# One more block of a GRU step by seven products instead of eight, in a four-layer graph network on one core

## The chip, the cores and the metric

The kernel runs on one core of a Trainium2 chip. A core has a matrix engine (PE, with its weight loads shown apart as PEld), a vector engine (DVE), an activation engine (ACT), a general engine (GpSimd, shown as POOL) and a queue from which transfers are issued (SP). Each engine works through its own queue in order; between engines semaphores hold an instruction until its inputs are there. The metric is device time in microseconds: 2803.21 us is the median of three runs of the kernel before (2800.3 to 2803.34).

## What is computed

128 graphs of 128 nodes with 256 features go through four layers, each followed by a layer normalisation of input plus output: an attention layer with four edge types, a mean-aggregation layer, three steps of a gated graph unit, and an attention layer. Cut to the third layer, which the change touches most:

```python
for i in range(3):
    m = h @ weight[i]
    aggr = A.T @ m                       # A = (adj != 0)
    gi = aggr @ w_ih.T + b_ih            # split in i_r, i_z, i_n
    gh = h @ w_hh.T + b_hh               # split in h_r, h_z, h_n
    r, z = sigmoid(i_r + h_r), sigmoid(i_z + h_z)
    n = tanh(i_n + r * h_n)              # the candidate; h_n is its state side
    h = (1 - z) * n + z * h
```

Everything is float32, with outputs of 128 x 128 x 256.

## The kernel before

Four graphs make a group (`G = 4`), 32 groups in all. Feature-major tiles hold 128 features on the partitions and the 512 nodes of a group in the columns (`T = 512`); 256 features are two such tiles (`KC = 2`). Per group the code records `loading`, `layer0`, `layer1`, `gru` with three calls of `step`, and `layer3`. The weights are prepared once in `weights`: `weight[i]` and `w_ih` are multiplied into `c_gi[i]`, so that a step needs only the aggregated state `agT` and the state `hT`.

**Order of the work.** Nothing is issued while it is recorded. Each operation becomes an `Op` with a cost, its predecessors and a nominal time (`paced`), and at the end of the file a planner issues them: at each turn it takes the engine that can start first, and on it, of the operations that are ready by its reckoning, the one with the earliest nominal time. `PERIOD` is the nominal distance of two groups; `EAGER` favours operations of the GRU on engines other than PE, `RUSH` the copies of `snapshot`; `HOP`, `PE_HOP` and `SLACK` are the margins that it adds between engines. Several groups are under way at once, so PE's queue mixes products of different groups and layers. All calls go to the engines through one helper, so every instruction of the trace carries line 232, and instructions are told apart by their tiles.

**A gate** (`gate`, line 701). A 256 x 256 weight block times the 256 x 512 state can be formed as 2 x 2 blocks. `direct` does this with products of 512 columns: two output banks, two products each. `gate` does it by Winograd's form of Strassen's scheme: seven products of 256 columns, with sums of weight blocks prepared in `w_s` and sums of state blocks formed by `sums` (on POOL for `hT`, tile `t_h`; on DVE for `agT`, tile `t_m`). Gates r and z add up state side and message side, so each of the seven is two products. The scheme accumulates products 1, 6, 7 and 4 in one PSUM bank, `shared`, and ACT copies it to SBUF after 1, 6 and 7 (`snapshot`, into quarters of `t_r` or `t_z`); products 5 and 3 go to a second bank, 2 to a third, and `plus` adds each to its quarter on DVE. A planner rule treats a PSUM bank as one thing: a product into a bank waits for whoever reads any part of it. There are eight banks, four under the tag `ps` and four under `gate`.

**The candidate.** Its state side is formed with `direct` into two banks of `ps`, and `hidden` moves them out with bias and factor 0.5 into tile `q`. Its message side is `direct` with `c_gi` and is added in `candidate`. `update` forms the new state, which `turned` and `back` turn into node-major form: DVE transposes 32 x 32 blocks into a tile `z_...`, SP stores it to DRAM and loads it back block-transposed. `turned_quick` does the same on PE and is used only in the first group and at the end.

**Normalising** (`normalise`, line 465). `statistics` gives mean and variance on DVE and the reciprocal root `rstd` on POOL. Graphs 0 and 2 of a group are then normalised on DVE and graphs 1 and 3 on ACT, in the tiles `xa`, `xb`, `xc` and `xd` of the four stages.

Of the kernel before, what the change touches and what calls it, by code (L numbers as in the profile page):

```python
# [18 lines left out]
def kernel(  # L19
# [219 lines left out]
    LANDING = 4.2  # L239
    HOP = 0.3  # L240
    PE_HOP = 1.0
    SLACK = 1.0

# [11 lines left out]
    def pool_cost(op, n, sums):  # L255
        return 1.56 if op in FAST else 0.55 if op == "memset" else 1.2 if n < 64 else 0.25 + n * 0.0023

# [7 lines left out]

    PERIOD = 92.637
    SPAN = 2.0
    EAGER, RUSH = 21.446, 39.26
    L0_START, L0_END, L1_START, L1_END, L3_START, L3_END = -2.0, -1.338, -0.867, -0.05, 0.05, 1.0
    H_END, M_START, M_END = 0.25, 0.12, 0.573  # L270

# [32 lines left out]

    w_s = tile_of("w_s", [P, NL + 1, 3, 2, P])

    def weights():
# [73 lines left out]
        for n in range(NL + 1):  # L381
            by = POOL if n > 1 else DVE
            w = [
                (w_hhT[:, k] if n == 0 else c_gi[:, n - 1, k])[:, : 4 * P].rearrange(
                    "p (g e x) -> p g e x", [P, 2, 2, P], g=2, e=2
                )
                for k in range(KC)
            ]
            a11, a12, a21, a22 = w[0][:, :, 0], w[1][:, :, 0], w[0][:, :, 1], w[1][:, :, 1]
            s2, s3, s4 = [w_s[:, n, j] for j in range(3)]  # L390
# [73 lines left out]

    def normalise(res, mv, rstd, tag):

        n = res.shape[1]
        nmr = tile_of(f"nmr_{tag}", [P, n], 2)
        DVE.scalar_tensor_tensor(nmr, mv[:, :, 0], -1.0, rstd, op0=OP.mult, op1=OP.mult)
        for b in range(0, n, 2):  # L470
            DVE.tensor_scalar(
                res[:, b, :], res[:, b, :], mv[:, b, 0:1], rstd[:, b : b + 1],
                op0=OP.subtract, op1=OP.mult,
            )
        for b in range(1, n, 2):
            ACT.activation(
                res[:, b, :], res[:, b, :], AF.Identity, bias=nmr[:, b : b + 1], scale=rstd[:, b : b + 1]
            )

    def softmax(alpha, tag, quick, tile=tile_of):  # L480

        n = alpha.shape[1]
        nmax = tile_of(f"nmax_{tag}", [P, n], 2)
        DVE.tensor_reduce(nmax, alpha, AX.X, OP.max, negate=True)
        p = tile(f"prob_{tag[0]}", [P, n, N])
        rs = tile_of(f"rsum_{tag}", [P, n], 2)
        for b in range(n):
            ACT.activation(
                p[:, b, :], alpha[:, b, :], AF.Exp, bias=nmax[:, b : b + 1], scale=1.0,
                accum_out=rs[:, b : b + 1],  # L490
            )
        rinv = tile_of(f"rinv_{tag}", [P, n], 2)
        DVE.reciprocal(rinv, rs)
        pT = tile(f"probT_{tag[0]}", [P, n, N])
        if quick:
            turned_quick(pT.rearrange(FLAT), [p[:, b, :] for b in range(n)])
        else:
            back(pT.rearrange(FLAT), turned(p, n, "p"))
        return pT, rinv
# [24 lines left out]
    def layer0(g, s):  # L524
# [39 lines left out]
        for h in range(G // 2):  # L564
# [5 lines left out]
            for j in range(2):  # L570
# [4 lines left out]
                )  # L575
        normalise(res, *statistics(res, "0"), "0")
        s.x1T = tile_of("x1T", [P, G, KC, N])
# [11 lines left out]
    def layer1(g, s):  # L589
# [17 lines left out]
        for b in range(G):  # L607
            ps = bank()
            PE.matmul(ps[:, : D + 1], a_f[:, b, :], hu[b][:, D:], start=True, stop=True)
            fac = tile_of("fac", [P, 1], 4)  # L610
            DVE.tensor_scalar_max(fac, ps[:, D : D + 1], 1.0)
            DVE.reciprocal(fac, fac)
            DVE.scalar_tensor_tensor(
                fac, ps[:, D : D + 1], 0.0, fac, op0=OP.is_gt, op1=OP.mult
            )
            DVE.scalar_tensor_tensor(
                res[:, b, :], ps[:, :D], fac, hu[b][:, :D], op0=OP.mult, op1=OP.add
            )
# [3 lines left out]
        normalise(res, *statistics(res, "1"), "1")  # L622

# [17 lines left out]
    def gru(g, s):  # L641
# [5 lines left out]
        def step(i, hT, parts):  # L647
# [30 lines left out]

            def sums(by, v, w, n, src, tag):

# [9 lines left out]
                def of(q):  # L690
                    block = lambda k, e: w[:, k, (q + e) * P : (q + e + 1) * P]
                    extra = lambda j: w_s[:, n, j, q // KC]
                    return {
# [6 lines left out]

            def gate(tag, q, sources):

                t = tile_of(tag, [P, 4, H])
                shared, other, last = bank("gate"), bank("gate"), bank("gate")

                def add(ps, p, first=False):
                    with PE:
                        for k, of in enumerate(sources):  # L710
                            PE.matmul(
                                ps[:, :H], *of(q)[p], start=(first and k == 0),
                                stop=(p in (2, 3, 4) and k == len(sources) - 1), skip_group_check=True,
                            )

                def snapshot(quarter):
                    ACT.copy(t[:, quarter], shared[:, :H])
                    ops[-1].rush = RUSH

                def plus(quarter, ps):  # L720
                    DVE.tensor_add(t[:, quarter], ps[:, :H], t[:, quarter])

                def tanh(out, in_, c):
                    ACT.activation(out, in_, AF.Tanh, bias=brz[:, q + c : q + c + 1], scale=0.5)

                add(shared, 1, True)
                snapshot(0)
                add(last, 2, True)
                plus(0, last)
                add(shared, 6)  # L730
                snapshot(1)
                add(other, 5, True)
                add(shared, 7)
                snapshot(3)
                plus(3, other)
                tanh(t[:, 3], t[:, 3], 1)
                add(shared, 4)
                tanh(t[:, 2], shared[:, :H], 1)
                add(other, 3)
                plus(1, other)  # L740
                halves = [t[:, 2 * c : 2 * c + 2].rearrange("p h n -> p (h n)") for c in range(KC)]
                tanh(halves[0], halves[0], 0)
                return halves[1], halves[0]

            def hidden(c, ps):
                t = tile_of("q", [P, T], 2)
                ACT.activation(t, ps, AF.Identity, bias=bhn[:, c : c + 1], scale=0.5)
                return t

# [34 lines left out]
            of_m = sums(DVE, agT, w_i, i + 1, agps, "t_m")  # L784
            t1, t0 = gate("t_r", R, (of_h, of_m))
            n1, d1 = candidate(1, direct(w_i, agT, C + 1), t1, q1)
            n0, d0 = candidate(0, direct(w_i, agT, C), t0, q0)
            z1, z0 = gate("t_z", Z, (of_h, of_m))
            update(1, z1, n1, d1)
# [11 lines left out]
        "rT": ("xs", 2), "xc": ("xa", 2), "wh": ("x_in", 1), "e": ("alpha0", 1), "alpha3": ("xT", 2),  # L801
        "prob_3": ("prob_0", 1), "probT_3": ("probT_0", 1), "xd": ("z_1", 1),
    }

    def layer3(g, s, first, last):
# [59 lines left out]
        pT, rinv = softmax(alpha, three, end, tile)  # L865
        normalise(x3, mv, rstd, two)

# [3 lines left out]
        for h in range(n // 2):  # L871
# [16 lines left out]
            )  # L888
        normalise(res, *statistics(res, three), three)
        SP.dma_start(out=out[g * G + first : g * G + last].rearrange("b n d -> n b d"), in_=res)  # L890
# [35 lines left out]
    def slot_at(buf, ahead=False):  # L926


        taken = slots.setdefault((buf.pool, buf.tag), [])
        done = sorted([b.free_at for b in taken if b.left == 0] + [0.0] * (buf.bufs - len(taken)))  # L930
        place = 0 if buf.pool is psum else buf.place.index(buf)
        return done[place] if place < (len(done) if ahead else min(1, len(done))) else None
# [96 lines left out]
```

## Time and profile before

| what | value |
|---|---|
| median of three runs | 2803.21 us |
| profiled execution, its own time | 2803.81 us |
| span of its profile (first to last instruction) | 2802.0 us |
| granted clock of PE, mean over the span | 0.990 |
| PE busy | 2741.4 us, 98% |
| DVE busy | 2351.3 us, 84% |
| ACT busy | 1552.1 us, 55% |
| POOL busy | 1349.1 us, 48% |
| traffic to and from HBM | 318.89 MB, 114 GB/s |

The page divides the span in 40 slices and gives, for each engine, tenths of busy time. The groups of instructions give a name as output tile, arrow, input tiles; for example `q<-ps,bhn` is the copy of the candidate's state side. The means that the page gives for matrix products overlap each other, because products are pipelined: the cost of a product is the distance between the starts of two that follow each other. Each product in float32 shows as two instructions.

The rows of the candidate's state side and of its copy out of PSUM are these, from the groups of instructions by form (busy us, mean ns of one, then idle time before):

| group | count | busy us | mean ns |
|---|---|---|---|
| PE `ps<-hT,w_hhT`, 512 columns | 512 | 242.3 | 601 |
| PE `ps<-h0T,w_hhT`, 512 columns | 256 | 115.9 | 593 |
| ACT `q<-ps,bhn`, 512 elements | 192 | 131.5 | 685 |
| DVE `xa<-xa,mv,rstd`, 256 elements | 64 | 50.1 | 791 |
| DVE `xb<-xb,mv,rstd`, 256 elements | 64 | 23.9 | 412 |

### The profile page before, as it was taken

The page shows a single profiled execution, that of the slowest core. Times are in us where ns is not written, and L with a number is a line of the kernel's source. Part 1 is how long each engine was busy: PE and PEld are TensorE (multiplying, and loading weights), DVE is VectorE, ACT ScalarE, POOL GpSimd, SP SyncE. Part 2 cuts the span into 40 slices and gives each one's busy share as a digit, 9 for nine tenths or more (in the row PEclk, how much of TensorE's full clock was granted, in tenths as well). Part 3 has the DMA queues.
Part 4 walks back from the last instruction along what each step waited for, and adds up shares of the span by engine and source line. Part 5 has one row for each costly group of instructions (what it writes and reads, how often), then busy time and mean ns, then how long its engine had stood idle before and what let it go on. Part 6 is the DMA issues. An engine that isn't in the chain of part 4 may idle for free.

```text
span 2802.0 us, 42709 instructions
## 1 busy us (share of the span) xinstructions
PE 2741.4 (98%) x13180; PEld 2030.5 (72%) x13180; DVE 2351.3 (84%) x5389; ACT 1552.1 (55%) x3512; POOL 1349.1 (48%) x1358
## 2 busy tenths in 40 slices
PE   8899999999999999999999999999999999999995
PEld 5677777777777777777777777777777777776663
DVE  5777889888888888889888888888888888888775
ACT  4454555555655555555555655555565555655554
POOL 4433545544455544555544455544555544454431
PEclk9999999999999999999999999999999999999996
DMA  5454556546555555555646555555555646555441
GB/s 118 107 105 98 118 125 129 113 99 132 121 125 126 115 107 125 121 125 124 120 100 131 118 126 127 115 109 124 117 126 126 119 101 131 108 116 117 95 87 48
DMA packets 1396626, 321.78 MB, mean 115 GB/s; under 512 B 1142064, under 2 KB 1387952, under 8 KB 1396400
## 3 DMA queue, kind: packets, MB, share of 16 engines
q1 hardware_dynamic: 1393952, 316.69, 54.0%
q10 hardware_dynamic: 2448, 2.36, 0.3%
q8 instruction: 107, 1.75, 0.3%
q14 instruction: 119, 0.97, 0.1%
HBM read 185.74 MB, written 133.15 MB: 114 GB/s over the span
## 4 chain that ended last, share of the span: by engine, by line
PE 95%; DVE 2%; ACT 1%; issue 1%; DMA 0%; POOL 0%; ACTq 0%; POOLq 0%; DVEq 0%
PE ps L232 54%; PE gate L232 41%; DVE t_r L232 0%; DVE rest L232 0%; DVE t_d L232 0%; ACT xs L232 0%; DMA acol<-in_L_gnn_a_dram 0%; DMA hn<-in_L_gnn_weight_dram 0%; ACT ps L232 0%; DVE xd L232 0%; POOL mk L232 0%; DVE hT L232 0%; DVE st L232 0%; DVE xb L232 0%; DVE t_z L232 0%
## 5 line engine op out<-in xcount | busy, mean ns | idle before, releaser
L232 PE MATMUL ps<-agT,c_gi 128*128 128x512 f32 x768 | 357.8, 592 | 0.0
L232 ACT COPY t_r<-gate 128x256 f32<-128x256 f32 x288 | 106.3, 369 | 348.4 <-PE gate L232 345.5
L232 POOL TENSOR_TENSOR rstd<-rstd,neg_half 128x4 f32<-128x4 f32 (+1 forms) x128 | 144.8, 1133 | 288.5 <-DVE rstd L232 281.0
L232 PEld LDWEIGHTS ps<-xs,xT 128*128 128x128 f32 x2048 | 247.8, 193 | 22.8 <-ACT agT L232 7.2
L232 PE MATMUL ps<-xs,xT 128*128 128x128 f32 x2048 | 253.3, 277 | 2.9 <-ACT xs L232 2.3
L232 PE MATMUL ps<-hT,w_hhT 128*128 128x512 f32 x512 | 242.3, 601 | 12.9 <-ACT wh L232 10.0
L232 POOL TENSOR_TENSOR t_d<-hT,t_n 128x512 f32<-128x512 f32 x128 | 173.1, 1353 | 164.3 <-ACT t_n L232 160.0
L232 PE MATMUL ps<-w_um,x1T 128*128 128x512 f32 x512 | 236.5, 594 | 2.2 <-ACT x1T L232 2.2
L232 PE MATMUL gate<-agT,c_gi 128*128 128x256 f32 x768 | 229.3, 380 | 1.4 <-ACT agT L232 1.4
L232 PE MATMUL gate<-t_h,w_hhT 128*128 128x256 f32 x768 | 229.0, 380 | 1.4 <-ACT t_z L232 1.4
L232 PE MATMUL gate<-t_m,c_gi 128*128 128x256 f32 x768 | 229.8, 381 | 0.0
L232 PE MATMUL gate<-t_h,w_s 128*128 128x256 f32 x768 | 228.5, 379 | 0.0
L232 PE MATMUL gate<-t_m,w_s 128*128 128x256 f32 x768 | 228.4, 379 | 0.0
L232 ACT ACTIVATE q<-ps,bhn 128x512 f32<-128x512 f32 x192 | 131.5, 685 | 171.5 <-PE ps L232 169.0
L232 PEld LDWEIGHTS ps<-agT,c_gi 128*128 128x128 f32 x768 | 145.8, 190 | 110.3 <-issue 101.2
L232 POOL TENSOR_TENSOR t_d<-h0T,t_n 128x512 f32<-128x512 f32 x64 | 86.0, 1344 | 281.0 <-ACT t_n L232 261.4
L232 ACT ACTIVATE xs<-xT,acol 128x512 f32<-128x512 f32 x256 | 173.9, 715 | 64.6 <-PE ps L232 58.3
L232 POOL TENSOR_SCALAR mk<-a_f 128x512 uint8<-128x512 f32 x128 | 193.5, 1519 | 15.3 <-DVE alpha L232 9.1
L232 DVE TENSOR_TENSOR t_r<-gate,t_r 128x256 f32<-128x256 f32 x288 | 120.1, 417 | 87.0 <-PE gate L232 54.4
L232 PEld LDWEIGHTS gate<-t_h,w_s 128*128 128x128 f32 x768 | 142.8, 190 | 65.3 <-issue 48.5
L232 DVE TENSOR_TENSOR t_z<-gate,t_z 128x256 f32<-128x256 f32 x288 | 119.9, 416 | 79.0 <-PE gate L232 54.3
L232 ACT COPY t_z<-gate 128x256 f32<-128x256 f32 x288 | 106.7, 370 | 141.0 <-PE gate L232 125.7
(194 smaller groups left out, 7111.4 us busy)
## 6 DMA issues: line engine op xcount, KB each, us to landing
way_h<-z_h SPq DMA_DIRECT2D x190, 256.0 KB, 2.6
hn<-way_h SPq DMA_DIRECT2D x760, 64.0 KB, 2.4
x_blocks<-in_x_dram SPq DMA_DIRECT2D x256, 64.0 KB, 2.3
x_in<-in_x_dram SPq DMA_DIRECT2D x32, 512.0 KB, 4.1
way_x<-xb SPq DMA_DIRECT2D x32, 512.0 KB, 3.2
way<-z SPq DMA_DIRECT2D x64, 256.0 KB, 2.7
way_p<-z_p SPq DMA_DIRECT2D x62, 256.0 KB, 2.3
probT<-way_p SPq DMA_DIRECT2D x248, 64.0 KB, 2.4
```

Source lines behind the costliest of these rows:

```text
L232: getattr(self.engine, name)(*[a.real() if isinstance(a, View) else a for a in args], **{k: a.real() if isinstance(a, View) else a for k, ...
```

## The change

- The state side of the candidate goes through `gate` too, with the state side as its only source: seven products of 256 columns into banks of tag `gate`, in place of four of 512 columns into banks of tag `ps`. `hidden` now copies the snapshots (256 elements each), and DVE adds with a factor 0.5 (`half_more`). `w_hhT` gets its block sums for three gates (`w_sh`) where it had two; those of `c_gi` keep two (`w_sm`).
- A gate uses two banks: product 2 goes into the first half of `other`, products 5 and 3 into the second, and one DVE add over the whole bank replaces two over halves.
- Graphs 0 and 2 are normalised on POOL, except in the first group (layers 0 and 1) and at the end of the last one (layer 3).
- All block transposes share one tag `z` of four tiles; the eight-block transpose of `xa` becomes two of four, each with its own store. The softmax writes its exponentials over `alpha`. In layer 1, ReLU and residual are done for two graphs at a time.
- The planner's constants are other ones, also its estimate for one-input operations on POOL.

```diff
-    HOP = 0.3
-    PE_HOP = 1.0
-    SLACK = 1.0
+    HOP = 0.235
+    PE_HOP = 0.55
+    SLACK = 0.873
...
-    PERIOD = 92.637
+    PERIOD = 82.744
-    EAGER, RUSH = 21.446, 39.26
+    EAGER, RUSH = 5.34, 0.516
...
     def turned(src, n, tag):
-        z = tile_of(f"z_{tag}", [P, n, P], 2 if tag == "h" else 1)
-        DVE.transpose(z, src)
         way = tile_of(f"way_{tag}", [n, P, P], 8 if tag == "2" else 4, F32, dram)
-        SP.dma_start(out=way.rearrange("n p c -> p n c"), in_=z)
+        for first in range(0, n, G):
+            z = tile_of("z", [P, G, P], 4)[:, : min(n, G)]
+            DVE.transpose(z, src[:, first : first + G])
+            SP.dma_start(out=way[first : first + G].rearrange("n p c -> p n c"), in_=z)
...
-    def normalise(res, mv, rstd, tag):
+    def normalise(res, mv, rstd, tag, quick):
...
-            DVE.tensor_scalar(
+            (DVE if quick else POOL).tensor_scalar(
...
-            DVE.scalar_tensor_tensor(
-                res[:, b, :], res[:, b, :], 0.0, x1[:, b, :], op0=OP.max, op1=OP.add
-            )
+            if b % 2 == 1:
+                two = slice(b - 1, b + 1)
+                DVE.scalar_tensor_tensor(res[:, two], res[:, two], 0.0, x1[:, two], op0=OP.max, op1=OP.add)
...
-            def gate(tag, q, sources):
+            def gate(tag, q, sources, copied, added, last=None):
                 t = tile_of(tag, [P, 4, H])
-                shared, other, last = bank("gate"), bank("gate"), bank("gate")
+                shared, other = bank("gate"), bank("gate")
...
+                add(shared[:, :H], 1, True)
                 snapshot(0)
+                add(other[:, :H], 2, True)
+                add(shared[:, :H], 6)
                 snapshot(1)
+                add(other[:, H:], 5)
+                add(shared[:, :H], 7)
                 snapshot(3)
+                added(t[:, 3], other[:, H:], t[:, 3])
+                if last:
+                    last(t[:, 3], t[:, 3], 1)
+                add(shared[:, :H], 4)
+                (last or copied)(t[:, 2], shared[:, :H], 1)
+                add(other[:, H:], 3)
                 halves = [t[:, 2 * c : 2 * c + 2].rearrange("p h n -> p (h n)") for c in range(KC)]
+                added(halves[0], other, halves[0])
...
-            q0 = hidden(0, direct(w_hhT, hT, C))
-            q1 = hidden(1, direct(w_hhT, hT, C + 1))
-            of_h = sums(POOL, hT, w_hhT, 0, hT, "t_h")
+            of_h = sums(POOL, hT, w_hhT, w_sh, hT, "t_h")
+            q0, q1 = gate("q", C, (of_h,), hidden, half_more)
```

More of the change, by code (lines that the diff above doesn't have):

```diff
@@ L255, in pool_cost @@
     def pool_cost(op, n, sums):
-        return 1.56 if op in FAST else 0.55 if op == "memset" else 1.2 if n < 64 else 0.25 + n * 0.0023
+        return 0.2 + n * 0.00266 if op in FAST else 0.55 if op == "memset" else 1.2 if n < 64 else 0.25 + n * 0.0023
     PE = Engine("PE", nc.tensor, pe_cost)
@@ L263 @@
     engines = (PE, DVE, ACT, POOL, SP)
-    PERIOD = 92.637
+    PERIOD = 82.744
     SPAN = 2.0
-    EAGER, RUSH = 21.446, 39.26
-    L0_START, L0_END, L1_START, L1_END, L3_START, L3_END = -2.0, -1.338, -0.867, -0.05, 0.05, 1.0
-    H_END, M_START, M_END = 0.25, 0.12, 0.573
+    EAGER, RUSH = 5.34, 0.516
+    L0_START, L0_END, L1_START, L1_END, L3_START, L3_END = -2.032, -1.293, -0.75, -0.05, 0.173, 0.919
+    H_END, M_START, M_END = 0.179, 0.179, 0.503
     def paced(start, end, pe_only=False):
@@ L303 @@
     w3x = tile_of("w3x", [P, KC, 2 + D])
-    w_s = tile_of("w_s", [P, NL + 1, 3, 2, P])
+    w_sh = tile_of("w_sh", [P, 3, 3, P])
+    w_sm = tile_of("w_sm", [P, NL, 3, 2, P])
     def weights():
@@ L381, in weights @@
         for n in range(NL + 1):
-            by = POOL if n > 1 else DVE
+            by, gates = POOL if n > 1 else DVE, 3 if n == 0 else 2
             w = [
-                (w_hhT[:, k] if n == 0 else c_gi[:, n - 1, k])[:, : 4 * P].rearrange(
-                    "p (g e x) -> p g e x", [P, 2, 2, P], g=2, e=2
+                (w_hhT[:, k] if n == 0 else c_gi[:, n - 1, k])[:, : 2 * gates * P].rearrange(
+                    "p (g e x) -> p g e x", [P, gates, 2, P], g=gates, e=2
                 )
@@ L388, in weights @@
             ]
+            w_s = w_sh if n == 0 else w_sm[:, n - 1]
             a11, a12, a21, a22 = w[0][:, :, 0], w[1][:, :, 0], w[0][:, :, 1], w[1][:, :, 1]
-            s2, s3, s4 = [w_s[:, n, j] for j in range(3)]
+            s2, s3, s4 = [w_s[:, j] for j in range(3)]
             by.tensor_sub(s3, a11, a21)
@@ L484, in softmax @@
         DVE.tensor_reduce(nmax, alpha, AX.X, OP.max, negate=True)
-        p = tile(f"prob_{tag[0]}", [P, n, N])
         rs = tile_of(f"rsum_{tag}", [P, n], 2)
@@ L488, in softmax @@
             ACT.activation(
-                p[:, b, :], alpha[:, b, :], AF.Exp, bias=nmax[:, b : b + 1], scale=1.0,
+                alpha[:, b, :], alpha[:, b, :], AF.Exp, bias=nmax[:, b : b + 1], scale=1.0,
                 accum_out=rs[:, b : b + 1],
@@ L495, in softmax @@
         if quick:
-            turned_quick(pT.rearrange(FLAT), [p[:, b, :] for b in range(n)])
+            turned_quick(pT.rearrange(FLAT), [alpha[:, b, :] for b in range(n)])
         else:
-            back(pT.rearrange(FLAT), turned(p, n, "p"))
+            back(pT.rearrange(FLAT), turned(alpha, n, "p"))
         return pT, rinv
@@ L575, in layer0 @@
                 )
-        normalise(res, *statistics(res, "0"), "0")
+        normalise(res, *statistics(res, "0"), "0", g == 0)
         s.x1T = tile_of("x1T", [P, G, KC, N])
@@ L618, in layer1 @@
             )
-            DVE.scalar_tensor_tensor(
-                res[:, b, :], res[:, b, :], 0.0, x1[:, b, :], op0=OP.max, op1=OP.add
-            )
-        normalise(res, *statistics(res, "1"), "1")
+            if b % 2 == 1:
+                two = slice(b - 1, b + 1)
+                DVE.scalar_tensor_tensor(res[:, two], res[:, two], 0.0, x1[:, two], op0=OP.max, op1=OP.add)
+        normalise(res, *statistics(res, "1"), "1", g == 0)
         s.way_x2 = tile_of("way_x2", [P, G, D], 4, F32, dram)
@@ L677, in step, with sums @@
             H = T // 2
-            def sums(by, v, w, n, src, tag):
+            def sums(by, v, w, w_s, src, tag):
                 t = tile_of(tag, [P, 4, H])
@@ L691, in of @@
                     block = lambda k, e: w[:, k, (q + e) * P : (q + e + 1) * P]
-                    extra = lambda j: w_s[:, n, j, q // KC]
+                    extra = lambda j: w_s[:, j, q // KC]
                     return {
@@ L699, in sums, with add @@
                 return of
-            def gate(tag, q, sources):
+            def gate(tag, q, sources, copied, added, last=None):
                 t = tile_of(tag, [P, 4, H])
-                shared, other, last = bank("gate"), bank("gate"), bank("gate")
-                def add(ps, p, first=False):
+                shared, other = bank("gate"), bank("gate")
+                def add(cols, p, first=False):
                     with PE:
@@ L711, in add @@
                             PE.matmul(
-                                ps[:, :H], *of(q)[p], start=(first and k == 0),
-                                stop=(p in (2, 3, 4) and k == len(sources) - 1), skip_group_check=True,
+                                cols, *of(q)[p], start=(first and k == 0),
+                                stop=(p in (3, 4) and k == len(sources) - 1), skip_group_check=True,
                             )
                 def snapshot(quarter):
-                    ACT.copy(t[:, quarter], shared[:, :H])
+                    copied(t[:, quarter], shared[:, :H], quarter // 2)
@@ L718, in snapshot @@
                     ops[-1].rush = RUSH
[L720 to L726, printed above, removed]
+                add(shared[:, :H], 1, True)
                 snapshot(0)
-                add(last, 2, True)
-                plus(0, last)
-                add(shared, 6)
+                add(other[:, :H], 2, True)
@@ L731, in gate @@
+                add(shared[:, :H], 6)
                 snapshot(1)
-                add(other, 5, True)
-                add(shared, 7)
+                add(other[:, H:], 5)
+                add(shared[:, :H], 7)
                 snapshot(3)
[L735 to L740, printed above, removed]
-                halves = [t[:, 2 * c : 2 * c + 2].rearrange("p h n -> p (h n)") for c in range(KC)]
@@ L742, in gate @@
[L742 to L748, printed above, removed]
+                added(t[:, 3], other[:, H:], t[:, 3])
[3 more added lines that the diff above has]
+                (last or copied)(t[:, 2], shared[:, :H], 1)
@@ new lines, in gate, with copy, hidden, half_more @@
+                add(other[:, H:], 3)
+                halves = [t[:, 2 * c : 2 * c + 2].rearrange("p h n -> p (h n)") for c in range(KC)]
+                added(halves[0], other, halves[0])
+                if last:
+                    last(halves[0], halves[0], 0)
+                return halves
+            def copy(out, in_, c):
+                ACT.copy(out, in_)
+            def hidden(out, in_, c):
+                ACT.activation(out, in_, AF.Identity, bias=bhn[:, c : c + 1], scale=0.5)
+            def half_more(out, in0, in1):
+                DVE.scalar_tensor_tensor(out, in0, 0.5, in1, op0=OP.mult, op1=OP.add)
@@ L750, in candidate, with tanh @@
+            def tanh(q):
+                return lambda out, in_, c: ACT.activation(
+                    out, in_, AF.Tanh, bias=brz[:, q + c : q + c + 1], scale=0.5
+                )
             def candidate(c, ps, t, q):
@@ L783, in step @@
             paced(at + M_START - 0.03, at + M_START, True)
-            of_m = sums(DVE, agT, w_i, i + 1, agps, "t_m")
-            t1, t0 = gate("t_r", R, (of_h, of_m))
+            of_m = sums(DVE, agT, w_i, w_sm[:, i], agps, "t_m")
+            t0, t1 = gate("t_r", R, (of_h, of_m), copy, DVE.tensor_add, tanh(R))
             n1, d1 = candidate(1, direct(w_i, agT, C + 1), t1, q1)
             n0, d0 = candidate(0, direct(w_i, agT, C), t0, q0)
-            z1, z0 = gate("t_z", Z, (of_h, of_m))
+            z0, z1 = gate("t_z", Z, (of_h, of_m), copy, DVE.tensor_add, tanh(Z))
             update(1, z1, n1, d1)
@@ L801 @@
         "rT": ("xs", 2), "xc": ("xa", 2), "wh": ("x_in", 1), "e": ("alpha0", 1), "alpha3": ("xT", 2),
-        "prob_3": ("prob_0", 1), "probT_3": ("probT_0", 1), "xd": ("z_1", 1),
+        "probT_3": ("probT_0", 1), "xd": ("x1T", 1),
     }
@@ L865, in layer3 @@
         pT, rinv = softmax(alpha, three, end, tile)
-        normalise(x3, mv, rstd, two)
+        normalise(x3, mv, rstd, two, end)
         res = tile("xd", [P, n, D])
@@ L888, in layer3 @@
             )
-        normalise(res, *statistics(res, three), three)
+        normalise(res, *statistics(res, three), three, end)
         SP.dma_start(out=out[g * G + first : g * G + last].rearrange("b n d -> n b d"), in_=res)
@@ L930, in slot_at @@
         done = sorted([b.free_at for b in taken if b.left == 0] + [0.0] * (buf.bufs - len(taken)))
-        place = 0 if buf.pool is psum else buf.place.index(buf)
+        place = 0 if buf.pool is psum or buf.tag == "z" else buf.place.index(buf)
         return done[place] if place < (len(done) if ahead else min(1, len(done))) else None
```

## The prediction

> **What bounds the kernel now.** I read the page first (engine shares, slices, chain), then busy time by stretch, the groups by form, the matrix queue in order of time, and the waits.
>
> ```profile
> PE 2741.4 (98%) x13180; PEld 2030.5 (72%) x13180; DVE 2351.3 (84%) x5389; ACT 1552.1 (55%) x3512; POOL 1349.1 (48%) x1358
> ...
> PE   8899999999999999999999999999999999999995
> ...
> PEclk9999999999999999999999999999999999999996
> ...
> PE 95%; DVE 2%; ACT 1%; issue 1%; DMA 0%; POOL 0%; ACTq 0%; POOLq 0%; DVEq 0%
> ```
>
> The matrix engine (PE) is busy almost everywhere and is 95% of the chain that ended last. The stretches say where it is not:
>
> ```profile
> 486.00:2602.00 2116.00, 2113.99 (x10218) 1571.98 (x10217) 1835.48 (x4198) 1204.15 (x2734) 1053.09 (x1049) 1.00 0.57 119
> 2602.00:2700.00 98.00, 94.44 (x431) 68.03 (x430) 76.18 (x165) 50.65 (x117) 41.46 (x40) 1.00 0.47 98
> 2700.00:2740.00 40.00, 29.81 (x131) 21.74 (x130) 31.75 (x67) 20.42 (x42) 19.14 (x18) 0.89 0.43 93
> ```
>
> Columns: stretch, length, then busy time of PE, its weight loads, DVE, ACT, POOL, then clock, DMA share, GB/s. Over 2116 us in the middle PE idles 2 us, at full clock. The same view gives 20 us idle in the first 160 us, and 38 us after 2602. A group of four graphs takes 84.0 us (the same 6.04 us piece of the chain of waits begins at 972.18, 1056.23 and 1140.13). So PE time saved is time saved, as long as no other engine needs over some 82.7 us a group (84.0 - 39.6 / 32, below). In the middle DVE needs 1835.5 x 84.0 / 2116 = **72.9 us a group**, ACT 47.8, POOL 41.8.
>
> **What the change takes from PE.** Busy nanoseconds of matmuls overlap, so I use distances between starts. Columns: start, length, instruction; each product is two instructions.
>
> ```profile
> 1408.14 0.59 PE L232 MATMUL gate<-h0T,w_hhT 128*128 128x256 f32 x2
> 1408.58 0.59 PE L232 MATMUL gate<-agT,c_gi 128*128 128x256 f32 x2
> 1409.01 0.59 PE L232 MATMUL gate<-t_h,w_hhT 128*128 128x256 f32 x2
> 1409.44 0.59 PE L232 MATMUL gate<-t_m,c_gi 128*128 128x256 f32 x2
> 1409.87 1.88 PE L232 MATMUL ps<-agT,c_gi 128*128 128x512 f32 x4
> 1411.59 0.59 PE L232 MATMUL ps<-h0T,w_hhT 128*128 128x512 f32 x1
> ```
>
> Four 256-column products take 1409.87 - 1408.14 = 1.73 us, 0.4325 each; two 512-column ones take 1.72, 0.86 each. State side of the candidate, per step: before 2 banks x 2 = 4 products of 512, 3.44 us; after 7 of 256, 3.03 us. That is 0.4125 us x 96 steps (32 groups x 3) = **39.6 us**. Nothing else changes PE's work: both gates keep fourteen products each.
>
> Here a rule speaks against the change. The Trainium skill (TensorE: Matmul & The Clock Gate, "Back-to-back issue gap") says that with a weight load for every matmul both set the spacing, with 131 ns at 512 columns and 81 at 128: half the columns don't give half the time. Between those points 256 columns would be 98 ns, 0.75 of 512; the seven products would then cost 7 x 0.75 x 0.86 = 4.5 us, 1.07 us a step more, +103 us in all (an estimate from that page). The rows above have 0.503, since a load of 190 ns fits under the 216 ns of one 256-column instruction. I take the rows.
>
> **What it puts on the other engines**, per group:
> - DVE, q: each step gains a 256- and a 512-element add out of PSUM, by the rows of `t_r<-gate,t_r` (0.417) and `t_r<-t_r,ps` (0.685): 1.10 x 3 = +3.3. Gates r and z: three adds of 0.417 become 0.417 + 0.685, -0.15 x 6 = -0.9.
> - DVE, normalisations: two each of xa, xb, xc, xd leave (0.791, 0.412, 0.406, 0.420): -4.06. ReLU plus residual in pairs: 4 x 0.440 to 2 x about 0.69, -0.4. The transpose of x1 in two: +0.15. **Sum -1.9: 71.0 of 82.7 us**, 86% as now (87%).
> - ACT: two `q` of 0.685 become four of 256 elements, by `t_r<-gate,brz` 0.473: +0.52 x 3 = 1.6: 49.4.
> - POOL: eight normalisations of 256 elements. Before has no such row; `mk` is nearest, same operation at 512, 1.52 us. Half of it is 0.76; the other end is 1.52, should two operations with pointer operands cost double. I take 0.76: +6.1, 48 of 82.7 (at the upper end 54).
> All of this costs nothing while it is under PE. The transposes share four buffers instead of having their own, and one more store per group goes to SP; SP's queue mostly waits for DVE. The exponentials overwrite `alpha`, so its next fill waits for the transpose too, a few us of a period of 84. The weight sums for a third gate widen four operations in the first 100 us from 256 to 384 elements. The first group and the end keep the old engine for normalising.
>
> **What the eight POOL operations hold up.** In the built order each pair stands right behind its own reciprocal root on POOL, so it waits for nothing new. Behind it are `t_h` (which q, r and z wait for), the two `t_d`, the masks or the splits of x: each 1.5 us later (3.0 at the upper end), on an engine that idles half the time. And they may block DVE. The Trainium skill (SBUF — State Buffer, "Who interferes with whom") says that a DVE instruction with two SBUF inputs and a GpSimd one that reads SBUF exclude each other for the whole instruction. The rows:
>
> ```profile
> L232 POOL TENSOR_SCALAR mk<-a_f x128: 1483/1503/2016, 15.8 to 2487.4; 128x512 uint8<-128x512 f32 x128
> ...
> L232 DVE SCALAR_TENSOR_TENSOR t_r<-t_r,q x192: 647/684/1501, 96.8 to 2759.5; 128x512 f32<-128x512 f32 x192
> ```
>
> (least/median/most.) By the timeline, 28 of these `t_r<-t_r,q`, with two SBUF inputs, began while `mk` ran: mean 0.72 us against 0.68 with POOL idle; 14 that began under `t_h`, a POOL tensor_tensor, took 1.17. Nor does `mk` grow: 1.516 with such a DVE operation inside it, 1.507 alone. So in this trace the rule holds for POOL's two-input operations and not for its one-input ones, which the normalisations are. By the rule DVE would lose up to 6.1 us a group (77 of 82.7, still under PE); by the rows nothing. I take the rows.
>
> **Hand-offs.** The candidate side becomes a chain: products 1, 6, 7 and 4 go into one bank, with an ACT copy after each of the first three, and product 3 waits for a DVE add. PE's queue is in order, so a late copy stops everything behind it. What one needs:
>
> ```profile
> 1502.87 0.59 PE L232 MATMUL gate<-t_m,w_s 128*128 128x256 f32 x2
> ...
> 1503.50 0.37 ACT L232 COPY t_r<-gate 128x256 f32<-128x256 f32 x1 [2.28 <-PE gate L232]
> ```
>
> The pair has passed at 1503.30 (the next begins), the copy ends at 1503.87: 0.57 us, some 0.7 with the longer activation of q, and up to 0.72 more behind one other ACT operation (`xs`). In the built order of the changed kernel, priced with the rows above, the work between two such products of q is 2.4, 1.54 and 1.54 us at the 5th percentile or better except 0 in a few of the last group. For r and z it is 1.73 after product 1 (as before), 1.3 after 6 (before 1.78), 0.87 after 7 (before the same). That covers the middle. With nothing between stand 14 against 3 before, mostly in the last 200 us; eleven more at 0.6 us are 7 us at most. PE idles for the last group's chain there anyway, and I take **+1** (ends 0 and 7). The two banks in place of three cost nothing: product 3 waited for the same add before. That add is longer (0.685 for 0.417), seen only at the end.
>
> **Sum.** Profiled execution 2803.8 (span 2802.0) - 39.6 + 1 = 2765.2. It lay 0.6 above the median of the runs, so **2765** for the median.
>
> **Rivals.**
> 1. *Part is given back* in the middle: a POOL normalisation does hold DVE on a path that PE needs, one 0.76 us collision a group, 24 us: 2765 + 24 = 2789; at half, 2777. For it: DVE at 86% is the next engine. Against it: the `mk` rows.
> 2. *The ends shrink too*: PE idles 58 us in the first 160 and the last 200 us, and the planner's new pacing orders them anew. A quarter less: 2765 - 15 = 2750. For it: q no longer occupies two of the four general banks; against it: the built order puts the last group's three rounds of aggregation as far from the end in PE work as before (96, 55 and 27 us, both times).
> 3. *Slower*: hand-offs stall PE all through. There are 96 x 4 new ones and 192 x 4 old ones with less between, 1152; the gain is gone at 39.6 / 1152 = 34 ns each, or when one in ten waits 0.35 us, half an ACT operation. At 45 ns: +52 - 40, 2816. For it: planner margins are cut (PE's from 1.0 to 0.55) and copies lose their precedence (39.3 to 0.5). Against it: the order still leaves 0.87 us or more in the middle, where 0.6 to 0.7 is needed.
> 4. *No change* by under 0.2% (5.6 us, about what a measurement of this kernel can tell): rival 3 at half its price.
>
> **Numbers.** Forecast 0.66 (2757 to 2773), rival 1 0.15, rival 2 0.11, rival 3 0.05, rival 4 0.03. Faster: 0.66 + 0.15 + 0.11 = 0.92; same 0.03; slower 0.05. The range runs from rival 2 (2748) to rival 1's full price (2788) and leaves out the slower cases and the tails.
>
> **What will show it.** Right: `ps<-hT,w_hhT` at 512 columns gone, PE in the middle idle under 1%, period near 82.7, DVE some 71 us a group, POOL's normalisations near 0.76 and two-input DVE rows no longer than now. Wrong: 256-column products more than 0.44 us apart; PE waiting on ACT copies of `q`, `t_r` or `t_z` in the middle; DVE's `t_r<-t_r,q` near 1 us under POOL's `xb`; or the tail after the last group's first aggregation well off its present length.

## The result, and the profile after

The changed kernel takes **2764.05 us** (median of four runs, 2763.28 to 2765.23) against 2803.28 for the kernel before, run beside it: ratio 0.9862, 95% interval 0.9844 to 0.9879. The forecast was 2765. The profiled execution spans 2761.8 us, 40.2 less than before.

The page of the kernel after, busy time by engine and the chain of waits:

```profile
PE 2702.3 (98%) x13756; PEld 2138.1 (77%) x13756; DVE 2304.1 (83%) x5108; ACT 1584.2 (57%) x3704; POOL 1666.2 (60%) x1606
...
PE 94%; DVE 3%; POOL 1%; ACT 1%; DMA 1%; issue 1%; ACTq 0%; POOLq 0%; DVEq 0%; SPq 0%
```

PE still sets the end, with 39 us less to do and more instructions: 256-column products in place of 512-column ones. The same stretch of 2116 us as before, and two pieces of the chain in order of time (start, length, what):

```profile
486.00:2602.00 2116.00, 2111.79 (x10838) 1683.42 (x10837) 1823.89 (x4033) 1249.08 (x2932) 1329.93 (x1271) 1.00 0.56 120
```

```profile
520.79 6.04 PE gate L232 x28
...
603.46 6.04 PE gate L232 x28
```

PE idles 4 us of 2116, and a group now takes 82.67 us. In that period DVE is busy 1823.89 x 82.67 / 2116 = 71.3 us, ACT 48.8, POOL 52.0. The spacing, PE in order of time:

```profile
1408.30 0.59 PE L232 MATMUL gate<-t_h,w_sh 128*128 128x256 f32 x2
1408.73 0.59 PE L232 MATMUL gate<-t_m,w_sm 128*128 128x256 f32 x2
...
1411.76 1.88 PE L232 MATMUL ps<-w_um,x1T 128*128 128x512 f32 x4
1413.48 0.59 PE L232 MATMUL gate<-t_h,w_hhT 128*128 128x256 f32 x2
```

0.43 us for a product of 256 columns, 0.86 for one of 512, as before.

PE's busy time hides short stalls: a pair of instructions of 256 columns shows as 0.59 us and costs 0.43, so a stall that fits into the difference counts as busy. For what follows I split each trace in another way. **Work** is the number of PE instructions of each form times the median distance of two that follow each other (216 ns at 256 columns, 429 at 512, 112 at 128, 56 in bf16). **Excess** is what the distances have beyond that, in the start (the first 470 us of work), the middle, and the end (the last 200 us of work). Some 15 us before the first and after the last product are outside of it. Each figure is good to about 1 us.

| kernel | time us | work | start | middle | end |
|---|---|---|---|---|---|
| before | 2803 | 2700 | 33 | 9 | 46 |
| after | 2764 | 2661 | 32 | 7 | 47 |
| candidate's products undone (e1) | 2834 | 2700 | 34 | 40 | 44 |
| before plus the products alone (e2) | 2860 | 2661 | 46 | 86 | 53 |
| the same, new planner constants (f3) | 2803 | 2661 | 31 | 42 | 53 |
| before, new planner constants (f6) | 2851 | 2700 | 43 | 42 | 53 |
| after, old planner constants (e4) | 2866 | 2661 | 54 | 84 | 51 |
| after, only margins old (f1) | 2847 | 2661 | 43 | 71 | 57 |
| after, only pacing and precedence old (f2) | 2796 | 2661 | 39 | 32 | 50 |
| after, only PE's margin old (g3) | 2791 | 2661 | 41 | 30 | 45 |
| after, normalising on DVE (e3) | 2795 | 2661 | 39 | 30 | 48 |
| the same, other constants (g4) | 2786 | 2661 | 35 | 18 | 55 |
| the same, yet other constants (h1) | 2787 | 2661 | 37 | 23 | 53 |
| message side by seven products too (g1) | 2961 | 2622 | 57 | 197 | 71 |

The first two rows are the result: work fell by 39.2 us (96 steps times 8 x 429 - 14 x 216 ns) and excess stayed. All others have more excess than either.

### The profile page after: what moved, and what is told of

It reads as the page before. It is cut to its first block, busy times and chain, and to the rows that moved or that the text cites. A ratio compares the mean times of both kernels' runs of the same rounds, so it can differ in the third digit from the quotient of the medians.

```text
span 2761.8 us, 44048 instructions
## 1 busy us (share of the span) xinstructions
PE 2702.3 (98%) x13756; PEld 2138.1 (77%) x13756; DVE 2304.1 (83%) x5108; ACT 1584.2 (57%) x3704; POOL 1666.2 (60%) x1606
## 4 chain that ended last, share of the span: by engine, by line
PE 94%; DVE 3%; POOL 1%; ACT 1%; DMA 1%; issue 1%; ACTq 0%; POOLq 0%; DVEq 0%; SPq 0%
PE gate L232 52%; PE ps L232 42%; DVE t_r L232 0%; POOL t_h L232 0%; DVE xb L232 0%; DVE st L232 0%; DMA rest<-in_L_gnn_w_hh_dram 0%; DVE z L232 0%; POOL rstd L232 0%; DMA hn<-in_L_gnn_weight_dram 0%; POOL xa L232 0%; DVE xa L232 0%; DVE t_d L232 0%; POOL t_d L232 0%; DVE hT L232 0%
## 5 line engine op out<-in xcount | busy, mean ns | idle before, releaser
L232 ACT ACTIVATE q<-gate,bhn 128x256 f32<-128x256 f32 x384 | 183.0, 477 | 314.4 <-PE gate L232 313.1
L232 PE MATMUL gate<-t_h,w_hhT 128*128 128x256 f32 x1152 | 345.2, 381 | 5.7 <-ACT t_z L232 4.3
L232 PE MATMUL gate<-t_h,w_sh 128*128 128x256 f32 x1152 | 337.1, 383 | 4.2 <-ACT q L232 1.7
L232 PEld LDWEIGHTS gate<-t_h,w_sh 128*128 128x128 f32 x1152 | 213.7, 191 | 62.8 <-issue 30.4
L232 PEld LDWEIGHTS gate<-t_h,w_hhT 128*128 128x128 f32 x1152 | 211.7, 191 | 56.1 <-issue 16.3
L232 PE MATMUL gate<-t_m,w_sm 128*128 128x256 f32 x768 | 228.4, 379 | 0.0
L232 PE MATMUL gate<-hT,w_hhT 128*128 128x256 f32 x768 | 222.8, 385 | 5.6 <-DVE hT L232 5.6
L232 POOL MEMSET hu<- 128x1 f32 x128 | 10.3, 96 | 303.8 <-DVE fac L232 224.5
L232 DVE TENSOR_TENSOR t_z<-gate,t_z 128x256 f32<-128x256 f32 x192 | 104.2, 543 | 101.4 <-ACT t_z L232 53.7
L232 PEld LDWEIGHTS gate<-hT,w_hhT 128*128 128x128 f32 x768 | 141.8, 191 | 48.1 <-issue 23.6
```

Source lines behind the costliest of these rows:

```text
L232: getattr(self.engine, name)(*[a.real() if isinstance(a, View) else a for a in args], **{k: a.real() if isinstance(a, View) else a for k, ...
```

## The experiments

**One part alone, one part undone.** e1 gives `q` back to `direct`:

```diff
+            def outright(c):
+                t = tile_of("q", [P, T], 2)
+                hidden(t, direct(w_hhT, hT, C + c), c)
+                return t
...
-            q0, q1 = gate("q", C, (of_h,), hidden, half_more)
+            q0, q1 = outright(0), outright(1)
```

> The changed kernel with one part undone: the state side of the candidate again by four products of 512 columns into two general banks, copied out whole. POOL normalising, two-bank gates, shared transposes and the new planner constants stay. Theory P (PE sets the time, only the products changed its work): the whole 39 us come back, 2803 us, period 84.0. Rival O (the lighter DVE and the new planning bring part of the gain): clearly under the kernel before, 2785 to 2795 us.

In this run `direct` reads a block of `w_hhT` in which the preparation has put a sum of two blocks, so the state side is formed with other weights; number and shape of its products and copies are those of the kernel before. e2 is the kernel before with the block sums for a third gate and with `gate`, of three banks, for `q`; for it the snapshots are made by `hidden` and the adds have a factor 0.5:

```diff
-            q0 = hidden(0, direct(w_hhT, hT, C))
-            q1 = hidden(1, direct(w_hhT, hT, C + 1))
-            of_h = sums(POOL, hT, w_hhT, 0, hT, "t_h")
+            of_h = sums(POOL, hT, w_hhT, w_sh, hT, "t_h")
+            q1, q0 = gate("q", C, (of_h,), True)
```

> The kernel before with one part added: the state side of the candidate by seven products, in gates of three banks as before; normalising on DVE, old transposes, old planner constants. Theory P: 2764 to 2770 us, PE busy 2702, period 82.7; the other parts are worth at most a few us. Rival O: DVE now carries 1.25 us a step more (two adds of 256 and one of 256 more out of PSUM) with nothing taken off it, so 72.9 + 3.8 = 76.7 us a group of 82.7, 93%, and with the old margins PE waits for its copies: 2780 us or more.

Measured: e1 2834.13 us (ratio to before 1.0109, 1.0094 to 1.0124), e2 2860.43 (1.0202, 1.0185 to 1.0219). Undoing the products gives 31 us more than the kernel before, which neither theory had. The products alone make it **slower by 56 us**, although PE's work is the 2661 us of the changed kernel: theory P falls, and rival O's figure is far exceeded, with DVE at 88% of the middle. The waits of PE in the middle of e2 (waiting engine and tile, awaited; us in total, times, longest):

```profile
PE gate L232 <- DVE t_z L232: 17.9, 14, 1.7
PE gate L232 <- DVE q L232: 13.2, 13, 2.2
PE gate L232 <- ACT t_z L232: 9.6, 18, 1.0
```

In the first and the last row a gate waits for itself: product 3 for DVE's add, product 4 for ACT's copy. In the second, products 1 and 5, the first into their bank, wait for DVE's adds of `q`, which still read it: a gate takes three of the four banks here. In the kernel before PE shows no wait in this stretch. What the change to two banks is worth by itself was not run.

**The planner's constants.** e4 puts all of them back in the changed kernel, f1 and f2 parts of them:

```diff
-    HOP = 0.235                       # e4, f1: 0.3
-    PE_HOP = 0.55                     # e4, f1: 1.0
-    SLACK = 0.873                     # e4, f1: 1.0
-    PERIOD = 82.744                   # e4, f2: 92.637, with the windows of before
-    EAGER, RUSH = 5.34, 0.516         # e4, f2: 21.446, 39.26
```

> The changed kernel with all planner constants of the kernel before (pacing, margins, precedence of copies, the price of a one-input POOL operation); the operations are the same, only their order differs. Theory P: the middle stays full, 2764 to 2772 us, a difference only in the first 160 and the last 160 us. Rival O: PE waits on hand-offs in the middle, idle there over 1% instead of 0.2%, 2785 us or more.

2865.87 us (1.0221, 1.0206 to 1.0236): rival O's side, with the same instructions as the kernel of 2764. Then the parts:

> The changed kernel with only the three margins of the planner put back (0.3, 1.0 and 1.0 for 0.235, 0.55 and 0.873); pacing, precedence and the price of POOL stay new. The run with all constants old lost 102 us, 77 of it in stalls of PE in the middle. Theory M (margins decide: larger ones place the same product elsewhere, and DVE falls behind): at least half the loss, 2815 us or more. Theory W (pacing and precedence decide; margins on the safe side do no harm): 2764 to 2775 us.

> The changed kernel with only pacing and precedence put back (nominal period 92.6 for 82.7, the windows of the stages, the two precedence constants); margins and the price of POOL stay new. Theory W: at least half the loss, 2815 us or more, by waits of products 3 and 4 for DVE and ACT. Theory M: 2764 to 2775 us. Should both this and the run with old margins lose clearly, the constants work only as a set.

f1 2846.84 us (1.0156, 1.0141 to 1.0172), f2 2796.45 (0.9972, 0.9961 to 0.9983): the margins alone cost 83 us, pacing and precedence alone 32. One stall of f1, all engines in order of time:

```profile
1563.06 0.59 PE L232 MATMUL gate<-t_m,w_sm 128*128 128x256 f32 x2
1563.17 0.72 ACT L232 ACTIVATE t_r<-t_r,brz 128x512 f32<-128x512 f32 x1 [1.75 <-DVE t_r L232]
...
1563.80 0.71 ACT L232 ACTIVATE xs<-xT,acol 128x512 f32<-128x512 f32 x1
...
1564.51 0.72 ACT L232 ACTIVATE t_n<-t_r,bih 128x512 f32<-128x512 f32 x1
...
1565.14 0.35 ACT L232 COPY t_z<-gate 128x256 f32<-128x256 f32 x1
...
1565.54 0.70 PE L232 MATMUL gate<-t_h,w_hhT 128*128 128x256 f32 x2 [1.89 <-ACT t_z L232]
```

Product 7 has passed at 1563.5. Next in PE's queue, with nothing between, is product 4 into the same bank. Its copy of 0.35 us stands behind three activations on ACT and ends at 1565.5; PE stands for 2 us, once a group. Counted in the built orders, in the middle: f1 and e4 have 25 of 153 hand-offs from product 7 to 4 with no PE work between, one a group; before and after have none under 0.87 us. Not every stall is of this kind, as f3 and f6 below will show. The other kind of stall, from e4:

```profile
1579.17 1.49 POOL L232 TENSOR_TENSOR t_d<-hT,t_n 128x512 f32<-128x512 f32 x1 [1.01 <-ACT t_n L232]
1579.44 1.24 DVE L232 SCALAR_TENSOR_TENSOR nmr<-mv,rstd 128x4 f32<-128x4 f32 x1
...
1581.84 1.57 POOL L232 TENSOR_TENSOR rest<-xb 128x512 f32<-128x512 f32 x1
...
1582.45 1.51 DVE L232 SCALAR_TENSOR_TENSOR t_r<-t_r,q 128x512 f32<-128x512 f32 x1
...
1584.59 0.42 DVE L232 TENSOR_TENSOR t_z<-gate,t_z 128x256 f32<-128x256 f32 x1
...
1585.07 0.70 PE L232 MATMUL gate<-hT,w_sh 128*128 128x256 f32 x2 [1.23 <-DVE t_z L232]
```

`nmr` has four elements a partition and needs 0.15 us alone; under a POOL operation with two inputs it takes 1.24. `t_r` takes 1.51 for 0.68 in the same way. DVE is 1.9 us late, the add of `t_z` with it, and product 3 waits 1.23 us. Such losses are in every run here; whether PE sees them depends on where the order has put product 3.

To see whether the count of short hand-offs tells anything, g3 puts back one margin, `PE_HOP = 1.0`, which makes 20 of 153 zero:

> The changed kernel with one planner constant put back, PE's margin of 1.0 for 0.55. In the built order 20 of 153 hand-offs from product 7 to product 4 in the middle then have no PE work between, where the changed kernel has at least 0.87 us everywhere. Theory S: each costs the latency of a copy and what stands before it on ACT, 0.6 to 2 us as in the runs with old margins, so 2776 to 2805 us, and the wait shows at gate<-t_h,w_hhT for ACT. Rival (the count of short hand-offs tells nothing): within 4 us of 2764.

2791.03 us (0.9951, 0.9936 to 0.9966), and the wait is at `gate<-t_h,w_hhT` for ACT: about 18 us of the 30 in the middle. The count was a fair sign here.

**Operations and constants, crossed.** f3 is e2 with the new constants, f6 the kernel before with nothing but them:

> The kernel before plus the seven products for the candidate, now with all the new planner constants: gates of three banks, normalising on DVE, ReLU graph by graph. With the old constants this was 2860 us. Theory S (PE's products and a plan that fits are all; POOL normalising and two banks matter only as far as the plan fits them): 2770 to 2800 us, near the 2795 of the changed kernel with normalising on DVE. Rival O (DVE, now 76 of 82.7 us a group, cannot keep up under any plan): over 2815 us.

> The kernel before with nothing changed but the planner constants, all new. PE work is that of before, 84.0 us a group, so no plan can bring it much under 2795. Theory S: the new constants are no gain by themselves, 2800 to 2840 us; the 2834 of the run with the candidate undone points there. Rival N (the new plan is better for any kernel, mostly at start and end): 2785 to 2798 us.

f3 2802.59 us (0.9995, 0.9987 to 1.0004), f6 2851.43 (1.0168, 1.0152 to 1.0185):

| | old constants | new constants |
|---|---|---|
| operations of before | 2803 | 2851 |
| before plus the products | 2860 | 2803 |
| operations of after | 2866 | 2764 |

Neither set of constants is the better one: the old ones are good with the operations of before, the new ones with those of after. f6 came out slower than theory S said. f3 came in just over what S said, with all 39.2 us of work gone and none of the time.

Both also show what the count of short hand-offs misses. In their built orders every such place of the middle (products 1 to 6, 6 to 7, 7 to 4) has at least 0.86 us of PE work between, and yet each has 42 us of excess there. In f3, 28 of them stand before products that wait for DVE, mostly product 3 for the add of `t_z` and product 6 for the sums `t_m`; DVE is busy 89% of that stretch. In f6, 39 stand before products into `ps`, mostly those that wait for DVE's `t_r` and `t_m`. So rival O's number for f3 (over 2815) failed, but DVE is mostly what PE waits for there.

**Normalising on POOL.** e3, g4 and h1 have `DVE.tensor_scalar` in `normalise` for all groups; g4 and h1 also move constants:

```diff
-    HOP = 0.235                          # g4: 0.235       h1: 0.27
-    PE_HOP = 0.55                        # g4: 0.85        h1: 0.7
-    EAGER, RUSH = 5.34, 0.516            # g4: 10.0, 0.516 h1: 15.0, 2.0
```

> The changed kernel with normalisations of graphs 0 and 2 back on DVE. Theory P: DVE rises by about 8 x 0.41 = 3.3 us to 74.6 of 82.7 us a group, POOL falls by 8 x 1.22 = 9.8, and the time stays within 4 us of 2764. Rival O (unloading DVE is what makes the gain possible): PE idles 0.5 us a group or more, 2780 us or more. Rival L (POOL's normalisations cost DVE time by shutting it out): a few us faster, 2755 to 2760.

> The changed kernel with normalising on DVE, as in the run that took 2795 us, but with two planner constants moved (PE's margin 0.85 for 0.55, eager precedence 10 for 5.34) so that in the built order hand-offs 6 to 7 have 1.7 us between instead of 1.3 and hardly any 7 to 4 is under 0.87. Theory S (the 31 us were lost by an order that did not fit, not by DVE's load): 2765 to 2778 us. Rival O (DVE at 90% cannot follow; moving its work to POOL is a part of the gain): 2785 us or more.

> The changed kernel with normalising on DVE and four planner constants moved (margins 0.27 and 0.7, precedences 15 and 2), so that the built order has in the middle the same least PE work between hand-offs as the changed kernel: 1.73 us from product 1 to 6 and from 6 to 7, 0.87 from 7 to 4 in 26 of 153 and never less. Theory S (a fitting order is all that normalising on DVE lacked): 2764 to 2772 us, at most 10 us of excess in the middle as in the changed kernel. Rival O (DVE at 89% of a period falls behind under this order too; moving work to POOL is a part of the gain): 2780 us or more, with stalls of 0.2 to 0.3 us where PE waits for copies that stand behind DVE's work.

e3 2794.77 us (0.997, 0.9958 to 0.9981), g4 2785.92 (0.9936, 0.9919 to 0.9952), h1 2787.46 (0.9938, 0.9922 to 0.9955). In e3 theory P and rival L fail, and rival O has the number; 13 of the 30 us in its middle stand before products that wait for DVE. In g4 and h1 theory S failed by the numbers. But in h1 what rival O said of the cause is not what the trace has. The longest waits of PE's weight loads in the middle of h1:

```profile
PEld ps L232 <- ACT xs L232: 7.3, 24, 0.3
PEld gate L232 <- POOL t_h L232: 6.0, 23, 0.3
PEld ps L232 <- DVE xd L232: 5.7, 24, 0.2
```

The first is a hand-off of layer 0, once a group: PE frees a buffer of `xs`, ACT fills it, PE needs it. It makes 10 of the 23 us in the middle, and it is in no count of mine, which took gates only. It does not come from normalising on DVE: f2, which normalises on POOL, has the same stall, 24 times and up to 0.28 us each. Only 2 of the 23 us stand before products that wait for DVE. The other two rows are in the changed kernel as well (6.0 and 5.7 us), under other work. And of the 25 us by which its span is longer, 10 are in the start and the end. So three orders with normalising on DVE lost 22 to 31 us; that none could reach 2764 is not shown, and the worth of this part stays **open**.

**Further in the same direction.** g1 forms the message side of the candidate by seven products too:

```diff
-            n1, d1 = candidate(1, direct(w_i, agT, C + 1), t1, q1)
-            n0, d0 = candidate(0, direct(w_i, agT, C), t0, q0)
+            c0, c1 = gate("t_c", C, (of_m,), copy, DVE.tensor_add)
+            n1, d1 = candidate(1, c1, t1, q1)
+            n0, d0 = candidate(0, c0, t0, q0)
```

> The changed kernel carried further: the message side of the candidate too by seven products, from sums of blocks that are there already for r and z, six PSUM banks for gates and two for the rest, margins 1.0 and 1.0, three transpose buffers. PE work falls by another 96 x 0.4125 = 39.6 us; DVE rises by one add of 256 and one of 512 a step, 3.3 us a group, to 74.5 of 81.4 (92%), ACT by four copies of 256, 4.5, to 53. In the built order no hand-off in the middle has less than 0.86 us of PE work between (product 7 to 4: 0.87 in 25 of 150, as in the changed kernel). Theory S (PE work is the floor, and an order without short hand-offs reaches it): 2725 to 2735 us. Rival O (DVE over 90% with its lock losses cannot follow): 2750 us or more, PE waiting for DVE adds.

2960.83 us (1.056, 1.0544 to 1.0576), the slowest of all with the least work. Rival O has the number, but DVE is not full (81% of the span). The waits of PE:

```profile
PE ps L232 <- DVE alpha L232: 46.0, 19, 3.9
PE gate L232 <- ACT q L232: 23.8, 15, 1.8
PE ps L232 <- issue: 23.6, 12, 2.0
PE ps L232 <- DVE xd L232: 22.1, 19, 2.7
```

Of the 197 us in the middle 134 stand before products into `ps`. The largest group, 39 us, are products of layer 3 (`ps<-wh,probT`) that wait for `alpha` of layer 0, 12 times and up to 3.3 us: they take nothing from it, so what they can wait for is a bank. Gates have six of the eight banks here, and all other layers share two. That two are too few is argued from these waits, not shown: margins, `PERIOD` and the number of transpose buffers moved in the same run, and a split of five to three was not run. No version here beats the changed kernel.

## Why the prediction was right, step by step

- **PE bound, work falls by 39.6.** 39.2 by the distances in the traces, 39.2 by the medians of the runs. This term carried the whole result.
- **Spacing at 256 columns.** 216 ns over 7255 instructions, half of 429. The rule of the Trainium skill (TensorE: Matmul & The Clock Gate, "Back-to-back issue gap") that both loads and matmuls set the spacing would have made it 0.75 of the 512-column one, by the estimate in the prediction; it did not show.
- **Engine loads.** DVE forecast at 71.0, measured 71.3; ACT 49.4 and 48.8; POOL 48 and 52.0. The POOL term was mis-sized: the normalisation takes 1.22 us, not half of `mk`; it lies between the two ends that were given.
- **The lock.** The prediction said that POOL's one-input operations do not shut out DVE's two-input ones. That is too simple, see below, though it cost nothing here. Its mean of 0.72 us over 28 rows hid two kinds: 13 that began by 0.42 us into `mk` and waited 0.06 to 0.10, and 15 that began later and did not wait. The rows of the changed kernel, by tile (least, median, most):

```profile
L232 POOL TENSOR_SCALAR xb<-xb,mv,rstd x62: 1212/1224/2488, 125.4 to 2587.4; 128x256 f32<-128x256 f32 x62
...
L232 DVE TENSOR_TENSOR rest<-rest x128: 726/998/1842, 121.3 to 2702.3; 128x512 bf16<-128x512 f32 x128
```

 The median of `rest<-rest` was 746 ns before and is 998: it begins under `xa` or the cast of the adjacency on POOL 53 times of 128, and takes 0.99 and 1.04 us there against 0.74 with POOL idle. The sign that two-input DVE rows grow no longer thus failed for this row; PE's excess did not grow, so DVE's queue had room.
- **Hand-offs, +1.** Excess changed by -0.3 us at the start, -2.0 in the middle and +1.2 at the end, -1 together. The number is right, and g3 shows that the argument, work left between hand-offs in the built order, is a needed one. It is not enough: f3, f6 and h1 pass the same test with 23 to 42 us of excess in the middle. That the changed kernel has no stall of another kind was not derived; there the forecast was also lucky.
- **What the prediction took too lightly.** It gave rival 3 a chance of 0.05 and spoke of the constants as a risk to be checked in the order. The mechanism of that rival was dormant only because order and operations fit each other: e4, e2 and f1, with the same work, take 83 to 102 us more than the changed kernel, with stalls of 0.6 to 2 us a time. Its price (45 ns a hand-off for all 1152) was too evenly spread: what happens in f1 and e4 is one to three long stalls a group. Rival 1 (a collision with POOL each group) and rival 2 (start and end shrink) did not come. The ends of its range, 2748 and 2788, are 2 and 1 us off those rivals' own sums.

## What to carry to other kernels

Where one engine is busy 98% of the time, the work taken from it, priced by the distance of starts, is the forecast, but only for an order that keeps it fed: the same instructions took 2764 and 2866 us. So read the order that is built, at the places where a product needs a copy or an add of its own predecessor, and compare the work between with the latency of the copy plus what stands before it in that engine's queue; include the buffers of every stage, not only those that the change touches, and what DVE's own delays do to the adds that PE waits for. And constants of a planner that are good with one set of operations say nothing of another: do not judge an edit by them alone, nor by its gain in work alone.

## What was not expected of the hardware

A POOL operation with one input shuts out DVE's two-input operations only in its first part. In the changed kernel a DVE operation that began 0.21 us into a POOL normalisation waited 0.20 us, one that began at 0.41 waited 0.01; with `mk`, of twice as many elements, the edge lies at about 0.47 of 1.5 us (trace of before: begun at 0.02, waited 0.46; at 0.39, 0.08; at 0.72, none). Under a two-input POOL operation the wait lasts until some 0.13 us before that operation ends (trace of before, `t_h` with 0.68 us left: 0.56). It works the other way round, too; POOL and DVE of the changed kernel in order of time:

```profile
535.88 3.67 POOL L232 TENSOR_SCALAR xb<-xb,mv,rstd 128x256 f32<-128x256 f32 x2
...
536.12 1.28 DVE L232 SCALAR_TENSOR_TENSOR hT<-t_d,t_n 128x512 f32<-128x512 f32 x2
```

Two normalisations need 2 x 1.22 = 2.44 us alone and take 3.67: the first began while DVE ran three two-input operations in a row, and waited 1.2 us. So the rule of the Trainium skill (SBUF — State Buffer, "SBUF: two separate sides") that whichever starts first gets the shared port pair "for the whole instruction" fits POOL's two-input operations here but for the last 0.13 us, and not its one-input ones.
